# One register load per expert tile, and block 3's attention products traced ahead of block 2's tiles

## The chip, the cores and the metric

The kernel runs on one core of a Trainium2 chip, as one program in one launch. The metric is device time in microseconds (us): the median of repeated executions of the whole program. The kernel before takes 2506.33 us (five runs, 2505.71 to 2507.92).

The core has five engines that run side by side, each with its own instruction queue that is worked off in order: TensorE (PE: matmuls and transposes; its weight loads are listed as PEld), VectorE (DVE), ScalarE (ACT), GpSimd (POOL) and SyncE (SP). SP computes nothing: its queue reads registers and issues DMAs, which 16 DMA engines then carry out. POOL issues the indirect DMAs, those whose row numbers come from a tile.

## The reference

The input is x, 16 sequences of 128 tokens with 256 features. Four blocks follow each other; each adds a cross-attention to a context and then a feed-forward part, both gated by a tanh, both on the layer-normed x:

```
x = x + tanh(g_xattn[l]) * xattn_l(layernorm(x), ctx)
x = x + tanh(g_ffn[l])   * ffn_l(layernorm(x))
```

In blocks 2, 3 and 4 the feed-forward part is a mixture of experts: a router gives every token its K best experts (K = 2 of 8, 4 of 16, 8 of 64), and the token gets the weighted sum of these experts' outputs. One expert of block 2 or 3 is

```
h = silu(x @ Wg) * (x @ Wu)      # 256 -> 176
y = h @ Wd                       # 176 -> 256
```

Block 3's attention has 16 heads of 128 features and normalises queries and keys. Its output is the sum over the heads of attn @ v @ Wo, and since v = ctx @ Wv, the product Wv @ Wo of each head can be formed once from the weights alone. Everything is float32.

## The kernel before, in words

The functions run in the order of the blocks: xattn0, ffn0, xattn1, ffn1, xattn2, ffn2, xattn3, ffn3 (names count from 0; this text counts blocks from 1). The parts that matter are ffn1 (block 2's experts), xattn2 (block 3's attention) and ffn2 (block 3's experts).

**Routing.** While an attention part is running, `Routed.pieces` is worked off beside it, for two sequences at a time: layer norm, transposes (L460, copied by ACT at L468), logits (L158), the best K experts (L171 to L174), places in the experts' lists (L212, L213), target rows (L236), and then K indirect DMAs per sequence from POOL's queue (L240), which send each token's row to its experts' lists in DRAM (`xs_f`). The last pair of sequences is only done after the attention, in `r.finish()`.

**The tile table.** `sparse_experts` (L979 on) counts the tokens of each expert, and computes for each tile of 128 rows its expert and its first row: `tab` has one tile per partition and two columns. It is cast to integers in `tabi` (L1014). The expert number of every tile is also spread over all partitions, by a matmul against the identity (L1019) and a copy (L1021), as `ebc`.

**The tile loop.** There are 39 tiles in ffn1 and 79 in ffn2. Each tile goes through six steps that are staggered over the loop's turns:

- `load` (L1028): SP reads two registers from `tabi`, the expert (L1029) and the row (L1030), each with a check of its bounds; then it issues the load of the expert's up weights `wgu` (L1032, 352 KB, 5 buffers) and of the rows `xe` (L1034, 131 KB in ffn1, 134 KB in ffn2, 4 buffers)
- `load_down`: SP issues the load of the down weights `wdn` (L1040, 176 KB, 5 buffers), one turn later
- `turn`: PE transposes `xe` (L795), DVE copies the result to `xeT` (L1047) and finds the rows to send the results to (L262, L267, L269)
- `up`: matmul (L1054), ACT's silu (L1056), DVE's product (L1058)
- `turn_back`: PE transposes h (L1065), ACT copies it (L1067)
- `down`: matmul (L1074), DVE's weighting (L1076), POOL's indirect DMA of the result rows (L273)

The order of the queues of SP and PE is the written one inside the loop (`manual_schedule`). Everywhere else a planner orders each queue at compile time, by its own estimates and with the order of the program as priority: it may put an instruction far ahead of its place in the program as soon as its inputs and buffers are there. In the attention parts the queues of PE, DVE and ACT are written out by hand and those of SP and POOL are left to the planner.

In ffn2 the loop also carries the shared expert's work: `others` is a list of 40 pieces, the first 12 of which (`ahead`) are traced before the loop and the others spread over its turns. In ffn1 this list is empty.

**Between ffn1 and xattn2.** `xattn2` (L1143) begins with its weights: `wa` (Wq, 2 MB), `wc` (Wk, 1 MB), `wd` (Wv transposed, 1 MB in two halves, L1148), `wb` (Wo, 2 MB), then the 16 products of Wv and Wo in place (`value_products`, matmul at L570, ACT's copy back at L571, two PSUM banks by turns). Then it fetches the experts' results, which the last tiles must have sent (`fetch`, L281), adds them to x (L287), takes the layer norm and begins its own loop with L1163. Block 4 uses the tile `wd` again, for a constant (the load `wd<-in_sums`).

## Time and profile before

| what | value |
|---|---|
| median of five runs | 2506.33 us |
| the profiled execution: its own time | 2522.49 us |
| its span, first to last instruction | 2520.5 us |
| PE busy | 2029.3 us (81%) |
| DVE busy | 1486.2 us (59%) |
| mean granted PE clock | 0.909 of full speed |
| `wgu` loads of the two tile loops | 118 of 352 KB |
| PE busy in ffn1's tiles (811 to 944 us) | 111.72 of 133 us |
| PE busy in ffn2's tiles (1571 to 1831 us) | 244.49 of 260 us |

The page gives, for one profiled execution, the busy time of each engine and the granted PE clock in 40 slices of the span. The trace behind it can be asked for any stretch: which instruction ran when, what an engine's idle time ended with ("waits"), and the busy time of each engine in a list of stretches. Register reads, checks and DMA issues on SP are not counted as busy, but the trace lists each with its start and duration, so SP's queue has to be read from there. In the name of a load, the tile stands left of the arrow and its source right of it. Each float32 matmul of this kernel shows as two MATMUL records.

### The profile page before, as it was taken

The numbers are of one execution on the slowest core, as the hardware profiler recorded it, in microseconds if no ns is written. First come the engines' busy times: TensorE is split into PE (matmuls) and PEld (weight loads), VectorE is DVE, ScalarE is ACT, GpSimd is POOL, SyncE is SP. The second block draws the span as 40 slices with busy tenths as digits, with TensorE's granted clock in tenths as the row PEclk, the third lists the DMA queues.
The fourth block names the chain that finished last, engine by engine and source line by source line (L and its number), as shares of the span: only waits on it lengthen the run. The fifth ranks groups of instructions, "written<-read, shape, count | busy, mean of one in ns | idle before, by whom it ended". The sixth has DMA issues, their size and how long they took to land. (4 is left out here: it accounts for less than half of the span.)

```text
span 2520.5 us, 38199 instructions
## 1 busy us (share of the span) xinstructions
PE 2029.3 (81%) x12988; PEld 1421.4 (56%) x12988; DVE 1486.2 (59%) x4176; ACT 880.3 (35%) x1868; POOL 805.0 (32%) x799
## 2 busy tenths in 40 slices
PE   8999998798886886998999997999946877643760
PEld 5777764366564553665666664666635656533550
DVE  4676764488785444667666664555557745332438
ACT  3433333376562223454444442222223333111320
POOL 1121111243453232334444443223221144444430
PEclk9999999799897998999999998999978888666995
DMA  5169971129002771001000003787722011115768
GB/s 174 67 133 237 271 196 34 51 75 342 14 23 85 241 219 37 17 1 32 16 27 16 16 27 118 228 248 244 237 69 75 1 56 56 65 70 180 248 206 296
DMA packets 198528, 299.32 MB, mean 119 GB/s; under 512 B 21513, under 2 KB 151024, under 8 KB 195904
## 3 DMA queue, kind: packets, MB, share of 16 engines
q1 hardware_dynamic: 175776, 238.90, 33.1%
q0 software_dynamic: 19488, 55.31, 5.9%
q10 hardware_dynamic: 3072, 2.68, 0.3%
q8 instruction: 105, 1.72, 0.3%
q14 instruction: 87, 0.71, 0.1%
HBM read 160.92 MB, written 135.90 MB: 118 GB/s over the span
## 5 line engine op out<-in xcount | busy, mean ns | idle before, releaser
L548 POOL TENSOR_TENSOR e<-e,r 128x512 f32<-128x512 f32 x128 | 133.0, 1039 | 565.8 <-DVE r L547 284.9
L273 POOL DMA_INDIRECT y_f<-ys,drow x182 | 175.0, 961 | 399.2 <-DVE ys L1076 199.1
L240 POOL DMA_INDIRECT xs_f<-hx,hrow x224 | 221.8, 990 | 115.6 <-issue 56.8
L536 ACT ACTIVATE e<-e 128x512 f32<-128x512 f32 x128 | 80.7, 630 | 476.0 <-DVE e L533 476.0
L1054 PE MATMUL mm<-wgu,xeT 128*128 128x352 f32 x472 | 166.6, 476 | 8.7 <-DVE xeT L1047 6.0
L1163 PE MATMUL qk<-wa,xnT 128*128 128x512 f32 x256 | 130.0, 631 | 23.4 <-DVE nq L1177 23.3
L543 DVE TENSOR_REDUCE sm<-e 128x4 f32<-128x512 f32 x128 | 87.8, 686 | 93.2 <-ACT e L536 92.4
L795 PE MATMUL tr<-cst,xe 128*128 128x128 f32 x364 | 72.6, 282 | 79.4 <-DMA wgu<-in_L_gu 46.0
L1074 PE MATMUL o<-wdn,hT 88*128 88x256 f32 x472 | 122.7, 382 | 2.0 <-ACT hT L1067 2.0
L667 PE MATMUL y<-wb,aT 128*128 128x256 f32 x512 | 121.1, 379 | 1.0 <-DVE x_sb L415 1.0
L1216 PE MATMUL y<-wb,aT 128*128 128x256 f32 x512 | 120.9, 379 | 0.0
L667 PEld LDWEIGHTS y<-wb,aT 128*128 128x128 f32 x512 | 97.1, 190 | 41.8 <-issue 18.0
L633 PE MATMUL mm<-xnT,wm 128*128 128x512 f32 x256 | 120.0, 593 | 0.0
L795 PEld LDWEIGHTS tr<-cst,xe 128*128 128x128 f32 x364 | 46.2, 144 | 125.4 <-issue 93.4
L390 POOL TENSOR_TENSOR rr<-ss,nhalf 128x8 f32<-128x8 f32 x64 | 106.0, 1656 | 31.7 <-DVE ss L1171 31.6
L287 DVE TENSOR_TENSOR x_sb<-x_sb,yg 128x256 f32<-128x256 f32 x224 | 93.4, 423 | 32.7 <-DMA yg<-y_f 20.5
L1177 DVE TENSOR_TENSOR nq<-qk,rr 128x512 f32<-128x512 f32 x64 | 44.3, 692 | 113.2 <-POOL rr L390 113.2
L873 DVE TENSOR_REDUCE mx<-sc 128x4 f32<-128x512 f32 x128 | 84.6, 681 | 39.6 <-PE sc L866 39.6
L1067 ACT COPY hT<-tr 88x256 f32<-88x256 f32 x118 | 43.5, 368 | 183.3 <-PE tr L1065 183.1
L1054 PEld LDWEIGHTS mm<-wgu,xeT 128*128 128x128 f32 x472 | 81.8, 193 | 43.1 <-DVE xeT L1047 14.9
L521 PEld LDWEIGHTS tr<-cst,e 128*128 128x128 f32 x512 | 63.4, 141 | 69.9 <-issue 60.8
L1516 PE MATMUL mm<-xeT,wgu 128*96 128x128 f32 x512 | 71.7, 284 | 35.9 <-ACT ys L1530 24.2
(287 smaller groups left out, 4845.4 us busy)
## 6 DMA issues: line engine op xcount, KB each, us to landing
wgu<-in_L_W SPq DMA_DIRECT2D x118, 352.0 KB
xs_f<-zeros SPq DMA_DIRECT2D x32, 1072.0 KB
wdn<-in_L_W SPq DMA_DIRECT2D x118, 176.0 KB
xs_f<-zeros SPq DMA_DIRECT2D x16, 1048.0 KB
y_f<-zeros SPq DMA_DIRECT2D x16, 1024.0 KB
yg<-y_f SPq DMA_DIRECT2D x16, 1024.0 KB
wgu<-in_L_gu SPq DMA_DIRECT2D x64, 192.0 KB
xe<-xs_f SPq DMA_DIRECT2D x79, 134.0 KB
```

The lines of the kernel that those rows point to most:

```text
L240: ins = nc.gpsimd.indirect_dma_start(out=self.rows, out_offset=bass.IndirectOffsetOnAxis(ap=h["row"][:, j, k : k + 1], axis=0), in_=h["x"] ...
L273: self.net.unordered("y_" + self.name, self.net.nc.gpsimd.indirect_dma_start(out=self.y, out_offset=bass.IndirectOffsetOnAxis(ap=row, axis ...
L287: self.net.nc.vector.tensor_tensor(x, x, yg[:, k, :], ALU.add)
L390: return self.nc.gpsimd.tensor_tensor(out, var, self.nhalf[:, :n], ALU.pow)
L548: nc.gpsimd.tensor_tensor(e, e, r.unsqueeze(2).to_broadcast([P, 4, S]), ALU.mult)
L633: nc.tensor.matmul(mm, wm[:, kk, 4 * hq + j, :], self.xnT[:, kk, g * 512 : (g + 1) * 512], start=kk == 0, stop=kk == 1,)
L667: nc.tensor.matmul(y, a[:, j, :], wn[:, 4 * hq + j, :], start=j == 0, stop=j == 3)
L795: self.nc.tensor.transpose(tr[:, kk, :], src[:, kk * P : (kk + 1) * P], self.ident)
L1054: nc.tensor.matmul(gu, xeT[:, kk, :], wgu[:, kk, :], start=kk == 0, stop=kk == 1)
L1074: nc.tensor.matmul(y, hT[:, c, :], wdn[:, c, :], start=c == 0, stop=c == 1)
L1163: nc.tensor.matmul(q, self.xt(kk, b), wq[:, kk, cols], start=kk == 0, stop=kk == 1)
L1216: nc.tensor.matmul(y[b], a[:, j, :], wn[:, h, :], start=h == 0, stop=h == 15)
```

## The change

It has two parts.

**The register load.** The table is turned: `tabi` becomes one row on one partition, with expert and row of each tile side by side. For this a second small matmul against the identity turns the row column (`rp`), and two copies on one partition fill `tabi` from PSUM. In the loop one load instruction reads both registers of a tile, and the checks of their bounds are left out.

**The products.** Block 3's attention weights are loaded in a new function `weights2`, called at the start of `ffn1`, and the 16 products become `others` of ffn1's `sparse_experts` with `ahead` 16: they are traced after the tile table and ahead of the tile loop, with the PSUM banks `sc`, two of them.

```diff
-        tabi = self.sb(pool, "tabi", [P, 2], I32)
-        nc.vector.tensor_copy(tabi, tab)
...
+        rp = self.psum("mm", [1, T])
+        nc.tensor.matmul(rp, tab[:, 1:2], self.ident[:, 0:T], start=True, stop=True)
         ep = self.psum("mm", [P, T])
         nc.tensor.matmul(ep, wide, self.ident[:, 0:T], start=True, stop=True)
+        tabi = self.sb(pool, "tabi", [1, T, 2], I32)
+        nc.vector.tensor_copy(tabi[:, :, 1], rp)
+        nc.vector.tensor_copy(tabi[:, :, 0], ep[0:1, :])
...
         def load(i, _):
-            ev = nc.sync.value_load(tabi[i : i + 1, 0:1], min_val=0, max_val=E - 1)
-            rv = nc.sync.value_load(tabi[i : i + 1, 1:2], min_val=0, max_val=E * NT)
+
+            _, (ev, rv) = nc.values_load_multi_w_load_instructions(
+                tabi[0:1, i, :], engines=(mybir.EngineType.SP,), min_val=0, max_val=E * NT,
+                skip_runtime_bounds_check_because="the table's entries are clamped to the bounds",
+            )
+            ev = nc.s_assert_within(ev, 0, E - 1, skip_runtime_bounds_check_because="clamped to E - 1")
...
     def ffn1(self):
+        self.weights2()
+        products = [partial(self.value_product, "sc", self.w2[2][:, h, :], self.w2[3], h) for h in range(16)]
         with self.tc.tile_pool(name="f1", bufs=1) as one, self.tc.tile_pool(name="f1s", bufs=3) as sp:
-            self.sparse_experts(one, sp, self.t["L1_W1"], self.t["L1_W2"])
-    def xattn2(self):
+            self.sparse_experts(one, sp, self.t["L1_W1"], self.t["L1_W2"], products, 16)
+    def weights2(self):
         nc, t = self.nc, self.t
-        wq = self.weight("wa", t["L2_Wq"].rearrange("(k p) n -> p k n", p=P), [P, 2, 2048])
-        wk = self.weight("wc", t["L2_Wk"], [P, 2048])
         wvT = self.sb(self.wpool, "wd", [P, 16, P])
...
         wo = self.weight("wb", t["L2_Wo"].rearrange("(h p) n -> p h n", p=P), [P, 16, D])
-        wn = self.value_products("qk", wvT, wo, lambda h: h)
+        wq = self.weight("wa", t["L2_Wq"].rearrange("(k p) n -> p k n", p=P), [P, 2, 2048])
+        wk = self.weight("wc", t["L2_Wk"], [P, 2048])
+        self.w2 = wq, wk, wvT, wo
+    def xattn2(self):
+        nc, t = self.nc, self.t
+        wq, wk, _, wn = self.w2
```

## The prediction

> **What bounds the kernel now.** I read the table of stretches first: engine by engine, the busy time in block 2's tiles (between 811 and 944 us) and in block 3's (1571 to 1831 us). Columns: stretch, length, busy PE, PEld, DVE, ACT, POOL, then granted PE clock, DMA share, GB/s.

> ```profile
> 811.00:823.00 12.00, 10.53 (x29) 6.15 (x29) 4.53 (x18) 2.97 (x6) 0.00 (x0) 0.62 0.73 222
> 823.00:923.00 100.00, 83.65 (x373) 55.12 (x371) 48.91 (x186) 21.05 (x62) 29.79 (x31) 1.00 0.81 247
> ...
> 1571.00:1831.00 260.00, 244.49 (x1076) 167.66 (x1074) 137.87 (x484) 58.33 (x165) 74.76 (x78) 1.00 0.77 235
> ```

> No engine is full in block 2's tiles: PE is at 84% at full clock, DMA at 0.81. In block 3's tiles PE is at 94%. The waits say what PE lacks in block 2, between 811 and 932 us; the second line is SP's own, at the head of the loop:

> ```profile
> PE tr L795 <- DMA xe<-xs_f: 15.1, 20, 1.9
> ...
> SPq L1034 <- DMA xs_f<-hx,hrow: 3.5, 1, 3.5
> ```

> PE waits 15.1 us, in 20 tiles, for rows that come late. Late because SP asks late: the timeline of SP's queue shows one tile after the other without a pause for a buffer.

> ```profile
> 869.63 0.35 SPq L1040 DMA_DIRECT2D wdn<-in_L_W  x1
> 871.59 0.34 SPq L1032 DMA_DIRECT2D wgu<-in_L_W  x1
> 872.18 0.33 SPq L1034 DMA_DIRECT2D xe<-xs_f  x1
> 872.75 0.35 SPq L1040 DMA_DIRECT2D wdn<-in_L_W  x1
> 874.70 0.34 SPq L1032 DMA_DIRECT2D wgu<-in_L_W  x1
> ```

> One tile costs SP 874.70 - 871.59 = 3.11 us; with stops for buffers the mean from tile 2's wgu (812.94) to tile 38's (930.44) is 117.5/36 = 3.26. The gaps hold the register loads; the listing by line gives their parts (duration min/median/max in ns, start of first and last) for 869 to 875 us:

> ```profile
> L1029 SPq TENSOR_LOAD <-tabi x2: 492/500/507, 870.0 to 873.1; - x2
> L1029 SPq FUSED_REGOPS  x2: 152/154/155, 870.6 to 873.7; - x2
> ...
> L1030 SPq TENSOR_LOAD <-tabi x2: 274/277/280, 870.8 to 874.0; - x2
> L1030 SPq FUSED_REGOPS  x2: 157/157/157, 871.2 to 874.3; - x2
> ```

> From 870.0 to the next load's registers at 871.4 it is 1.4 us, nearly half of SP's turn. What PE could do without SP is at the loop's end, when every load has been issued:

> ```profile
> 930.17 0.38 PE L795 MATMUL tr<-cst,xe 128*128 128x128 f32 x2
> 930.39 1.03 PE L1074 MATMUL o<-wdn,hT 88*128 88x256 f32 x4
> 931.26 0.38 PE L1065 MATMUL tr<-cst,h 128*88 128x128 f32 x2
> 931.77 1.45 PE L1054 MATMUL mm<-wgu,xeT 128*128 128x352 f32 x4
> 933.06 0.38 PE L795 MATMUL tr<-cst,xe 128*128 128x128 f32 x2
> ```

> A turn is 2.89 us here (933.06 - 930.17), of which 0.39 is PE's weight load waiting for xeT, as the timeline says. So block 2's tiles are **SP-bound at 3.26 against 2.89**, and block 3's, which carry 28 pieces more for PE, are PE-bound with little idle.

> **Part 1, the register load.** *What SP saves.* Gone are one of two loads, both register operations and both assertions. At most it saves all but one load of 0.50: 0.9. At least nothing, if the second register costs its 0.28 again and the register operations stay. I take the nearest row, the first load's 0.50 plus 0.05 of gap, for the load of two, and the checks as gone: 1.4 - 0.55 = 0.85, so SP's turn becomes 3.26 - 0.85 = 2.41, no longer the bound.

> [...] The trace gives 0.50 and 0.28 for two single ones. [...]

> *What is late next.* PE's turn (2.89 as in the tail; 2.50 if DVE does xeT first and the 0.39 goes) or the DMA engines: at a share of 0.81 a tile takes 3.26, so at 1.00 it would take 0.81 x 3.26 = 2.64. I take 2.8, between 2.64 and 2.89.

> *Block 2.* The first transposes of the 39 tiles run from 810.48 to 935.95: 125.47 us, of which the first two turns (3.69 and 3.66) are at the clock of 0.62 and stay. New: 7.35 + 36 x 2.8 = 108.15. **Gain 17.3 us.** With 2.89 it is 14.1, with 2.64 it is 23.1. If only the second load's 0.3 goes, SP's 2.96 sets it: 125.47 - 7.35 - 36 x 2.96 = 11.6.

> *Block 3.* SP leads PE by its buffers here; PE's waits for xe are 7.1 us, 10 times, between 1560 and 1835. Part of that PE gives back to DVE's chain. **Gain 5 us**, ends 0 and 7.1.

> *The table.* Added per loop: a matmul and two copies, less one cast. By L1019 at the low clock (0.65 us) and L1021 (0.20): 0.65 + 2 x 0.20 - 0.17, and the wide copy (0.22) and both hand-overs now lie before SP's first read: some 1.7 us later. In block 2 this is hidden, since SP then stands 3.5 us for the scattered rows; in block 3 because PE works on shared pieces until 1570.8, while the first wgu is issued at 1551.28. **0 us**; without this cover 3.4 for both.

> **Part 2, the products.** *Taken from behind block 2's tiles.*

> ```profile
> 944.17 9.31 PE L570 MATMUL qk<-wb,wd 128*128 128x256 f32 x32 [0.58 <-DVE ys L1076]
> ...
> 947.66 5.06 SPq L281 DMA_DIRECT2D yg<-y_f  x4
> ...
> 960.52 0.72 PEld L460 LDWEIGHTS tr<-cst,xn 128*128 128x128 f32 x4 [7.44 <-DVE xn L447]
> ```

> The 9.31 us look like a stretch on the path, but PE then idles for 7.04 until the layer norm's rows come. Their chain goes past PE: last result rows sent by POOL at 944.39, fetched by SP at 947.66, added by DVE until 956.4, statistics, power on POOL, rows at 960.06. ACT is done with the products at 953.9 and first needed at 961.68. **0 us saved**; no gain, because nothing in that chain waits for them.

> [...]

> *Put ahead of block 2's tiles.* All 32 records need about 9.3 us at full clock. PE is busy 6.65 of 17 us from 786 to 803, and 0.52 of the 8 after it; the work fits, at a clock of 0.60 and 0.50. What it can hit is the routing of the last pair (L460 at 792.01, L158 at 793.85, L212 at 797.80), which ends in the scatter that the first xe waits for. Block 3's head shows the planner putting such pieces between these steps: there the second pair of L460 came 2.28 us after the first. Here a piece is one product, two records of 128x256, 0.96 at half clock (four of L1074's took 1.92 at 926.45), at three stops: +2.9; a PE kept busy does L158 in 0.96 instead of 1.88 and L460 in 0.63 instead of 1.11: -1.4. **+1.5 us**, ends -2 (the first two tiles at 2.8 too) and +15 (all in front, at half clock).

> *The weights.* Written earlier, but the planner has already put them at 400.07 (wb), 454.21 (wa), 457.90 (wd) and 91.0 (wc): 0 us. Behind the products hangs the load of the constant into wd (now 953.51). If it moves ahead of the tiles, SP's queue stands there until the last product is done, covered by the 3.5 us above.

> **Sum.** -17.3 - 5 + 0 + 0 + 1.5 = -20.8. The profiled execution takes 2522.49, its span 2520.5 and 1.99 around it; after: span 2499.7, time 2501.7. The median of the runs without a profile is 2506.33, 16.2 below the profiled time; the difference is carried over: **2485.5**.

> **Rivals.**
> - *DMA is the limit.* For: the share is the same 0.8 in both loops, and an xe takes 4.0 us to land (869.06 to 873.05) where the first took 2.2. Against: SP's queue hardly ever waits, and its instructions follow each other. A turn of 3.1 gives 125.47 - 7.35 - 111.6 = 6.5, block 3 nothing, +1.5: 2501.3.
> - *The load of two saves little.* 11.6 and 2 in block 3, +1.5: 2494.2.
> - *The products stand in front of the routing.* For: PE works in order and the planner fills gaps. Against: their priority is behind the routing's. +9.3 to +15 instead of +1.5: 2493 to 2499.
> - *The load of two is dearer than two loads* (the slower side). L1029's longest load took 0.965; two such are 1.93. It decides from a stretch over 1.4 us. At 0.5 more, SP's turn is 3.76 in block 2 (+18), 3.6 against 3.29 in block 3 (79 x 0.3 = +24), +1.5: 2550. Against: the second load took only 0.28.
> - *The products are not moved by the planner, or SP's loads not fused:* the first leaves 2484, the second 2508.

> **Chances.** Forecast case 0.52 (2476 to 2490), little saved 0.15, products in front 0.10, DMA 0.13, dearer load 0.05, not fused or anything else 0.05. About 0.2% (5 us) can be told from no change: faster 0.83 (the first three and half of DMA's), same 0.11, slower 0.06. The range reaches from 2476 (23.1 + 7.1 gained) to 2500, which leaves out half of DMA's case, the dearer load and the rest.

> **What would show it.** One TENSOR_LOAD per tile on SP of about 0.5 us and no assertions; SP's turn at 2.4, then stopping for buffers; PE's waits for xe under 4 us in block 2 and transposes 2.6 to 2.9 apart; DMA share near 0.9; the gap of 944 to 960 as long as now, without L570; the first xe issued within 2 us of 808.23. I am wrong if xe waits stay with SP ahead (DMA), if SP's turn stays above 2.9, or if the first xe is 5 us late.

## The result, and the profile after

The changed kernel is **slightly slower**: 2514.0 us at the median of 52 executions against 2509.76 of 91 of the kernel before on the same chip, a ratio of 1.0021 (95% interval 1.0013 to 1.0029). Forecast were 2485.5 us (2476 to 2500) with a chance of 0.06 for slower. The profiled execution took 2519.32 us, its span 2517.1.

Read by stages, it is two opposite results. The first transpose of an `xe` (L790 now, L795 before) and the last one bound each tile loop:

| stretch | before | after | difference |
|---|---|---|---|
| up to block 2's first transpose | 810.5 | 801.0 | -9.5 |
| block 2's tiles, first to last transpose | 125.5 | 106.5 | **-19.0** |
| from there to block 3's first transpose | 634.8 | 635.3 | +0.5 |
| block 3's tiles, first to last transpose | 253.1 | 280.2 | **+27.1** |
| the rest | 696.6 | 694.1 | -2.5 |

The first row is not the change's: in the runs below the same stretch took 797 to 805 us, with the products moved and without. It goes with the granted clock, which was 0.945 in it in the profile before and 0.966 in the one after. Of the programs without the products, PE was busy in this stretch for 715.3 us here, at 0.945, and in the runs below for 711.4 at 0.949 and 708 at 0.953 to 0.955. Without that row the profiled pair is near the medians: +6.1 against +4.2.

**Block 2's tiles went as forecast.** The table of stretches (length, busy PE, PEld, DVE, ACT, POOL, granted clock, DMA share, GB/s), two stretches of block 2's tiles and then block 3's, all after the change:

```profile
801.00:813.00 12.00, 10.82 (x28) 6.30 (x28) 3.94 (x18) 2.60 (x5) 0.00 (x0) 0.56 0.88 269
813.00:907.00 94.00, 92.70 (x414) 63.02 (x413) 51.36 (x208) 23.64 (x69) 32.59 (x34) 1.00 0.95 288
1543.00:1830.00 287.00, 253.49 (x1076) 174.85 (x1074) 128.93 (x482) 58.25 (x165) 74.58 (x78) 0.96 0.70 213
```

In block 2 PE rose from 84% to 92.70 of 94 us: it is the bound now, at a turn of 2.70 (median of the transposes' distances), and DMA follows close at 0.95. In block 3 the opposite happened: PE fell from 94% to 88%, and the DMA share from 0.77 to 0.70. SP's register load, from the listing by line for 860 to 872 us, and its queue after it:

```profile
L1028 SPq TENSOR_LOAD <-tabi x5: 697/744/752, 859.5 to 870.6; - x5
```

```profile
866.22 0.34 SPq L1034 DMA_DIRECT2D wgu<-in_L_W  x1
866.82 0.32 SPq L1036 DMA_DIRECT2D xe<-xs_f  x1
867.39 0.35 SPq L1042 DMA_DIRECT2D wdn<-in_L_W  x1
869.07 0.34 SPq L1034 DMA_DIRECT2D wgu<-in_L_W  x1
```

One load of 0.74 us instead of two (0.50 and 0.28), no register operations behind it and no assertions. The turn here is 2.85 us (869.07 - 866.22), but SP now stops for buffers within it, so this is no longer its own speed. That shows at the loops' heads, where SP stops for no buffer: the issues of `wgu` follow each other every 2.31 to 2.33 us there, against 2.98 to 3.01 before.

**The gap behind block 2's tiles is as long as it was**, as forecast: 26.7 us from the last transpose (907.5) to the first L1173 (934.23), against 26.7 before, with the products gone from it. The timeline shows the chain that keeps it:

```profile
915.75 0.96 POOL L273 DMA_INDIRECT y_f<-ys,drow  x1 [0.90 <-DVE ys L1078]
...
919.01 9.33 SPq L281 DMA_DIRECT2D yg<-y_f  x6
...
931.63 0.73 DVE L447 TENSOR_SCALAR xn<-x_sb,mv,rs 128x256 f32<-128x256 f32 x2 [1.30 <-POOL rs L390]
...
932.15 2.29 PE L460 MATMUL tr<-cst,xn 128*128 128x128 f32 x8 [17.20 <-DVE xn L447]
```

PE waits 17.20 us for the rows of the layer norm, where before it waited 7.44 and had done 9.31 us of products.

**Block 3's tiles lost more than block 2's gained.** The page, which counts the whole program, has a new group, the row of the store's destinations (busy, mean ns of one, idle before and its cause), and PE's up matmul shows idle time (before: 8.7):

```profile
L1056 PE MATMUL mm<-wgu,xeT 128*128 128x352 f32 x472 | 174.2, 494 | 33.8 <-DVE xeT L1049 33.2
...
L269 DVE TENSOR_SCALAR drow<-dw,cst 128x1 uint32<-128x1 f32 x182 | 38.8, 213 | 152.0 <-DMA y_f<-ys,drow 142.7
```

VectorE's waits in block 3's tiles (total, times, longest), after:

```profile
DVE drow L269 <- DMA y_f<-ys,drow: 99.6, 60, 3.3
DVE xeT L1049 <- PE tr L790: 33.0, 29, 2.7
```

and before:

```profile
DVE xeT L1047 <- PE tr L795: 17.0, 22, 1.2
...
DVE drow L269 <- DMA y_f<-ys,drow: 9.6, 12, 2.0
```

One such wait in the timeline after:

```profile
1641.01 0.15 DVE L267 TENSOR_REDUCE dw<-eq 128x2 f32<-128x8 f32 x1
...
1641.81 0.38 PE L790 MATMUL tr<-cst,xe 128*128 128x128 f32 x2
...
1643.87 0.21 DVE L269 TENSOR_SCALAR drow<-dw,cst 128x1 uint32<-128x1 f32 x1 [2.71 <-DMA y_f<-ys,drow]
1644.00 0.42 DVE L1049 COPY xeT<-tr 128x256 f32<-128x256 f32 x1
...
1644.47 1.45 PE L1056 MATMUL mm<-wgu,xeT 128*128 128x352 f32 x4 [1.19 <-DVE xeT L1049]
```

The transpose is done at 1642.2, but its copy `xeT` stands behind a `drow` in VectorE's queue, and `drow` waits for a store. PE gets its operand some 1.7 us late.

Why a store? `drow` has six buffers, used in turn. The scattered store of tile i-6 reads its row while it runs, so row i can only be written when that store has landed. In the trace after, the 60 waiting rows of block 3 began 3.4 us (median; 3.1 to 3.9 for the middle 80%) after the end of the issue of store i-6, and that issue takes 0.96: by this a store holds its row for some 4.4 us, an estimate. In the kernel before, the 61 rows that did not wait came 7.2 us (median) after it. What moved is the row's place in VectorE's queue. The order in which the two traces show the instructions, three turns of block 3, numbers relative to tile 31 (eq, drow: destination; h: product; ys: scaling, behind which POOL stores):

```
before: xeT(0) eq(1) ys(-3) drow(1) xeT(1) h(0) ys(-2) eq(2) drow(2) xeT(2) h(1) ys(-1) eq(3) drow(3) h(2)
after:  xeT(0) ys(-3) eq(3) xeT(1) h(0) ys(-2) drow(3) xeT(2) h(1) eq(4) ys(-1) drow(4) h(2) eq(5) drow(5)
```

Before, row 3 comes behind ys(-1), two scalings after ys(-3), whose store must have landed. After, it comes behind ys(-2), one scaling after, and ahead of xeT(2). Not every turn has this order, but the count over the loop says the same. Of the 73 rows from tile 6 on, 57 came behind the scaling of tile i-4 before the change, and none of these waited for a store; the other 16 came behind that of i-5 or i-6, and 12 waited. After, all 73 came behind that of i-5 (60 rows, 48 waited) or i-6 (13 rows, 12 waited). The loop's hand-written order holds SP and PE; VectorE's is the planner's.

### The profile page after: what moved, and what is told of

It is laid out like the page before. It is cut to its first block, busy times and chain, and to the rows that moved or that the text cites. A ratio compares the mean times of both kernels' runs of the same rounds, so it can differ in the third digit from the quotient of the medians.

```text
span 2517.1 us, 37642 instructions
## 1 busy us (share of the span) xinstructions
PE 2024.3 (80%) x12992; PEld 1423.1 (57%) x12992; DVE 1475.3 (59%) x4178; ACT 878.7 (35%) x1868; POOL 803.5 (32%) x799
## 4 chain that ended last, share of the span: by engine, by line
DVE 20%; PE 16%; issue 12%; DMA 9%; POOL 6%; ACT 4%; another core or an unknown queue 2%; SPq 0%; POOLq 0%; DVEq 0%; ACTq 0%
DMA y_f<-ys,drow 5%; POOL rr L390 4%; DVE x_sb L287 3%; DVE ss L1180 2%; POOL y_f L273 2%; DMA yg<-y_f 2%; PE mm L1056 2%; DVE e L533 2%; DVE sm L543 1%; DVE nq L1187 1%; ACT e L536 1%; PE mm L1526 1%; DVE mx L532 1%; PE sc L1374 1%
## 5 line engine op out<-in xcount | busy, mean ns | idle before, releaser
L1056 PE MATMUL mm<-wgu,xeT 128*128 128x352 f32 x472 | 174.2, 494 | 33.8 <-DVE xeT L1049 33.2
L1173 PE MATMUL qk<-wa,xnT 128*128 128x512 f32 x256 | 129.0, 627 | 24.1 <-DVE nq L1187 24.0
L269 DVE TENSOR_SCALAR drow<-dw,cst 128x1 uint32<-128x1 f32 x182 | 38.8, 213 | 152.0 <-DMA y_f<-ys,drow 142.7
L1076 PE MATMUL o<-wdn,hT 88*128 88x256 f32 x472 | 124.9, 388 | 2.0 <-ACT hT L1069 2.0
L790 PE MATMUL tr<-cst,xe 128*128 128x128 f32 x364 | 72.4, 282 | 54.3 <-DMA xe<-xs_f 54.2
L790 PEld LDWEIGHTS tr<-cst,xe 128*128 128x128 f32 x364 | 50.4, 146 | 91.9 <-issue 78.8
```

What stands on the lines that cost most here:

```text
L790: self.nc.tensor.transpose(tr[:, kk, :], src[:, kk * P : (kk + 1) * P], self.ident)
L1056: nc.tensor.matmul(gu, xeT[:, kk, :], wgu[:, kk, :], start=kk == 0, stop=kk == 1)
L1076: nc.tensor.matmul(y, hT[:, c, :], wdn[:, c, :], start=c == 0, stop=c == 1)
L1173: nc.tensor.matmul(q, self.xt(kk, b), wq[:, kk, cols], start=kk == 0, stop=kk == 1)
```

## The experiments

They ran on three other chips than the pair above (1 to 4 on one, 5 to 8 on one, 9 and 10 on one), which were granted a higher clock in the attention behind block 3's tiles (0.78 to 0.80 instead of 0.74); the kernel before takes 2452 to 2455 us on them. Times are therefore compared as ratios to the kernel before on the same chip.

**1. The load alone.** The kernel before with the changed table and load:

```
-            ev = nc.sync.value_load(tabi[i : i + 1, 0:1], min_val=0, max_val=E - 1)
-            rv = nc.sync.value_load(tabi[i : i + 1, 1:2], min_val=0, max_val=E * NT)
+            _, (ev, rv) = nc.values_load_multi_w_load_instructions(tabi[0:1, i, :], ...)
...
```

> The one register load per tile alone (with its new table); weights and products of block 3 stay where the kernel before has them. Theory (VectorE's queue): in block 3's tiles the destination row of tile i is written ahead of the copies of the two tiles before it, so it waits for the scattered store of tile i-6, which still reads the old row; that comes with the register load alone. So block 2's tiles are 19 us shorter, block 3's tiles 27 us longer, as in the changed kernel, and the 9.5 us of block 2's head are not there: about 2523 us, 0.5% above the kernel before, the drow line again with some 100 us of waits in block 3's tiles. Rival (the early weights or products disturb block 3): block 3's tiles stay at 253 us, the time is about 2491.

Measured: 1.0004 (0.9989 to 1.0019). Block 2's tiles 105.4, block 3's 276.5, with 95.7 us of waits of `drow` on stores in them. Both halves of the result come with the load and its table; the theory holds, and the rival (253 and 2491) does not. The expected 0.5% was too much by what the head was thought to be worth. In the trace, VectorE's order in block 3's tiles is the one of the changed kernel; that of experiment 2 is the one of the kernel before.

**2. The products alone.** The changed kernel with the old table and the two loads.

> The weights and products of block 3 moved, two register loads per tile as before. Theory: only the head of block 2's tiles is shorter (9.5 us, the products keep TensorE and its queue busy while the last pair is routed), both tile loops as before (125.5 and 253 us): about 2500 us, 0.4% below. Rival (products cost block 3): block 3's tiles near 280 us and about 2527. If the 9.5 us come from the register load instead: 2509, no change.

Measured: 0.9999 (0.9984 to 1.0014). Block 2's tiles 124.9, block 3's 255.7, first transpose 802.2. Moving the products shows no worth either way, within 0.15% (3.7 us). My 9.5 us for the head were wrong: see experiment 6.

**3. Twelve rows.** In the changed kernel:

```
-        dw = net.sb(self.sp, "dw", [P, 2], bufs=6)
+        dw = net.sb(self.sp, "dw", [P, 2], bufs=12)
-        row = net.sb(self.sp, "drow", [P, 1], U32, bufs=6)
+        row = net.sb(self.sp, "drow", [P, 1], U32, bufs=12)
```

> The changed kernel with 12 instead of 6 buffers of the destination rows and of their sums (dw), nothing else. Theory: a row is then written when the store of tile i-12 is long done, so the waits of drow on the stores (99.6 us in block 3's tiles) go to under 10 us, block 3's tiles take 253 us or less (27 us gained or more) and the kernel about 2485 us, 1% below the kernel before. Rival (transfers: with cheaper loads SP sends earlier, the stores and loads collide, and the waits are only where that shows): the wait moves to another line (eq on xe, or ys on its buffers), block 3's tiles stay near 280 us and the time near 2514.

Measured: **0.9836** (0.9813 to 0.9858). Block 3's tiles 244.2, without a wait of `drow` on a store; the group in that stretch, with its idle time last:

```profile
L269 DVE TENSOR_SCALAR drow<-dw,cst 128x1 uint32<-128x1 f32 x76 | 16.2, 213 | 2.2
```

The rival is out: the transfers could carry more (share 0.81 in this stretch, 0.71 in the changed kernel), and what was late were rows' buffers. More was gained than expected, since block 4's tiles, which call the same function, fell as well, to 132.2, from between 142.4 and 146.0 in runs 1, 2 and 5.

**4. The order held.** The changed kernel with six rows, and one word more:

```
-        with self.tc.manual_schedule(engines={mybir.EngineType.SP, mybir.EngineType.PE}):
+        with self.tc.manual_schedule(engines={mybir.EngineType.SP, mybir.EngineType.PE, mybir.EngineType.DVE}):
```

> The changed kernel with VectorE's order in the tile loops written out as well (each tile's copy, then its destination, in the order of the steps), six row buffers as before. Theory: the row of tile i is written one tile after the place where it stood in the changed kernel, behind the copy of tile i, three tiles' scalings behind; so no waits of drow on stores in block 3, block 3's tiles at 253 us or less and about 2485 us. It can cost a few us where the held order is a worse one for the other work in VectorE's queue: 2480 to 2497. Rival (transfers collide): near 2514 again.

Measured: **0.9831** (0.9803 to 0.9858). Block 3's tiles 238.4, block 4's 145.9 as before. Every row now stands behind its own tile's copy and the scaling of tile i-4. This takes the wait away without a buffer more: six rows are enough where a row stands behind the scaling of tile i-4, and too few where it stands behind that of i-5. PE in block 3's tiles:

```profile
1528.00:1768.00 240.00, 237.42 (x1057) 166.88 (x1056) 133.61 (x486) 56.82 (x161) 71.89 (x75) 1.00 0.84 260
```

It is busy for 237.4 of 240 us at a granted clock of 1.00: what is left of this loop is PE's own work. The held order also shortened the stretch from block 2's last transpose to block 3's first, which took 627 to 628 us in experiments 4, 7 and 10 against 633 to 635 in all other runs; the 7 us are gone between the last L1173 and block 3's first tile, and why was not tried.

**5. The changed kernel once more.**

> The changed kernel itself, for its profile and time on the same chip as the others. Theory: block 2's tiles 20 us shorter and block 3's tiles 24 to 27 us longer than in the kernel before: 0.2% above it; the first transpose of block 2's tiles near 802 us, as in the runs with the load alone and with the products alone. Rival (load and products together gain what neither gains alone): 0.3% below or better.

Measured: 1.0028 (1.0016 to 1.0039). Block 2's tiles 105.0, block 3's 272.2 with 98.9 us of waits of `drow`. The first result stands on a second chip; load and products together make nothing that the load alone does not.

**6. Twelve rows in the kernel before** (the edit of experiment 3).

> The kernel before with 12 buffers of the destination rows and of dw. Theory: in blocks 2 and 3 its rows hardly waited (9.6 us of waits in block 3's tiles, none in block 2's), in block 4 they did (50.8 us): block 2's tiles 125 us as they were, block 3's 247 to 253, block 4's near 133 instead of 146 to 148: 14 to 20 us less, a ratio of 0.992 to 0.994. So about 25 us of the 43 that the changed kernel with 12 rows is faster are the change's own. Rival (more rows do it all, whatever the loads): 0.984 here too. The first transpose of block 2 tells whether its head is 8 us longer without the products (810) or not (802).

Measured: 0.9947 (0.9932 to 0.9963). Block 2's tiles 124.2, block 3's 251.1, block 4's 130.2. So the rows help the kernel before almost only in block 4, where 50.8 us of waits stood already. First transpose at 800.6 without the products: the head does not depend on them.

**7. Both cures.** The changed kernel with the edits of experiments 3 and 4.

> The changed kernel with VectorE's order held in the tile loops of blocks 2 and 3 and with 12 buffers of the rows and of dw. Theory: the two cures meet in block 3 and only the rows act in block 4: block 3's tiles 238 us as with the held order, block 4's 132 as with the rows: 14 us under either alone, a ratio near 0.978. Rival (the transfers or the loads of SP take over): 0.983, with the DMA share at 0.9 and the waits of eq or xeT on xe in place of the others.

Measured: **0.9771** (0.9758 to 0.9785), the fastest run: 2398.47 us against 2453.11. Block 3's tiles 238.4, block 4's 133.0, both as expected.

**8. Eight rows.** The changed kernel with 8 buffers of `drow`, `dw` left at 6.

> The changed kernel with 8 instead of 6 buffers of the destination row alone (dw stays at 6). A store has landed some 3.4 us after its issue; in the changed kernel row i is written 3.4 us after the store of tile i-6 at the median, waiting, and never under 4.7 us after that of tile i-7. Theory: with the store of tile i-8 to wait for nothing waits, block 3's tiles at 244 and block 4's at 132 as with 12, a ratio near 0.984. Rival (the sums dw or a longer reach count too): 0.99 or more.

Measured: 0.9826 (0.9805 to 0.9846). Block 3's tiles 243.7, block 4's 129.8, no row waits for a store. Two buffers more, of one number per partition each, are as good a cure as twelve (0.9836 on its chip), and `dw` has no part in it.

**9. Four rows in the kernel before.**

> The kernel before with 4 instead of 6 buffers of the destination row, nothing else: the same mechanism brought into the kernel that did not have it. Theory: row i waits for the store of tile i-4, which in block 2 was issued after the last scaling before it on VectorE; scaling to landing is about 4.4 us (0.96 of issue and 3.4 after it), the row and the next scaling take some 0.6, so a turn cannot be under 5.0 us: block 2's tiles 38 x 5.0 = 190 instead of 125; in block 3 half of the rows stand behind one scaling more and cost nothing, the other half a turn of 5.0: 290 to 310 instead of 253; block 4 longer by 30 to 90. A ratio of 1.05 to 1.09. Rival (the row's wait covers a limit that is there anyway, such as the transfers): under 1.02.

Measured: 1.0278 (1.0249 to 1.0307). Both expectations missed the ratio. Block 2's tiles went from 125 to 148.9 and block 3's to 287.0, but block 4's stayed at 148.6. The waits of the row in block 2's tiles, where there were none before:

```profile
L269 DVE TENSOR_SCALAR drow<-dw,cst 128x1 uint32<-128x1 f32 x37 | 7.9, 214 | 82.6 <-DMA y_f<-ys,drow 82.5
```

The mechanism is there, and the size was off: in block 2 a waiting row began 2.1 us (median) after the issue of its store, not 3.4, so a turn took 3.8 and not 5.0 us. The landing time was not the same in both loops: in block 3's tiles of this run it was 2.8 us. Block 4 has another order in this trace: 62 of its 64 rows come behind the copy `xeT` of tile i-1, where with six buffers 52 come two copies earlier, behind that of i-3. Its waits for stores stayed at 50.6 us. So the planner gives way to fewer buffers in one loop and not in another (block 2's order is that of the kernel before); that this is why block 4 lost nothing was not tested.

**10. Both cures in the kernel before.**

> The kernel before with VectorE's order held in the tile loops and 12 buffers of the rows and of dw: what the change is worth when the rows hold nobody. Theory: SP's turn with two loads and three issues (3.1 us) is then what binds in both loops: block 2's tiles 125, block 3's 243 to 250, block 4's 131, a ratio of 0.990 to 0.995, so that the change is worth 1.3 to 1.8% beside the changed kernel with the same two cures (0.977). Rival (block 3 gains only from the held order): 238 in block 3 here too, and the change is worth block 2's 20 us alone, 0.8%.

Measured: 0.9921 (0.9897 to 0.9945). Block 2's tiles 124.9, block 3's 252.5, block 4's 131.5. Block 3 stays at 252.5 with the held order, a little over the theory's 243 to 250, and the rival's 238 is out: its 14 us there come from the load. With both cures in both kernels, the change is worth 0.9921 - 0.9771 = 1.5%, of which the spans show 18.2 us in block 2's tiles and 14.1 in block 3's.

## Why the prediction was wrong

- **Block 2: right.** Forecast 17.3 us of gain, measured 19.0 in the first pair and 19.5 between the runs of the load alone and the products alone. SP was the bound; behind it PE came first at 2.70 a turn (forecast 2.8), with DMA at 0.95 just after. The rival that DMA is the limit (6.5 us of gain) fell.
- **The register load: right in effect, mis-sized in its part.** I took 0.50 for the load of two; it takes 0.70 at the median over all 118. The two singles were 0.78 together, so the load itself saves under 0.1, and the rest of what SP saves is the checks and their gaps. By these medians the load of two takes 0.20 more than the first of the singles did. At the loops' heads the whole saving was some 0.7 a tile and not 0.85 (2.31 to 2.33 against 2.98 to 3.01). That cost nothing here, since PE's 2.70 was reached all the same.
- **Block 3: this step failed.** "Block 3. Gain 5 us, ends 0 and 7.1" became a loss of 27.1. The prediction read PE's waits for `xe` and counted what could go of them. It did not ask what holds VectorE's queue in this loop, although SP's and PE's orders alone are fixed there. With the new load the planner put the rows one scaling and one to two copies earlier, and six buffers no longer reached. Experiments 3, 4 and 8 take that away, each by another edit or another size, and then block 3's tiles take 244, 238 and 244. Beside the kernel before with the same edits (251 with twelve rows, 252.5 with both) that is a gain of 7 and 14 us, at my far end of 7.1 and beyond it. So the forecast's own quantity was there, and was turned into a new wait.
- **How the 27 us come about.** PE's idle time in block 3's tiles went from 253 - 238.5 = 14.5 to 280 - 247.5 = 32.5 us, 18 more; and its busy time grew by 9 at a granted clock of 0.96 instead of 1.00.
- **The gap behind block 2's tiles: right**, 0 saved (26.7 and 26.7).
- **The products ahead: +1.5 forecast, nothing that can be told from noise measured** (0.9999, within 0.0015 or 3.7 us, which leaves room for 1.5 and none for the far end of 15). They went into PE's idle time: ahead of block 2's first transpose PE is idle for 91 to 95 us in the five traces without them and for 84 to 88 in the seven with them. The load of the constant into `wd` did move ahead and SP stood 12.1 us behind the products, as the working feared; SP still waited 3.5 us for the scattered rows after that, so it was covered.
- **The table: 0 forecast**; the load alone with its table shows no cost at block 2's head (802.7 against 802.2 with the old table), though the spread of that stretch, 797 to 805 us, would hide the 1.7.
- **The rivals.** The slower side was given to one mechanism, a dear register load. The case that came was not among them: a buffer that is read by a transfer long after the engine that filled it has gone on (a store held its row for some 4.4 us, by the estimate above). It could have been seen. The trace of before has `drow` waiting for `y_f` in block 3's tiles, 9.6 us, and in block 4's, 50.8. A wait that small in a loop that one is about to make faster shows how near the limit is.

What stays open: why the planner moves the rows. That it does so with the load and its table, and not with the products, is in the orders that the traces show (experiments 1 and 2); whether the shorter load, the missing checks or the new table moves it was not tried.

## What to carry to other kernels

When a change makes one queue of a loop faster, look at every queue whose order is not written out: the planner may reorder it, and the new order has to be checked against the number of buffers of each small tile that a transfer reads. In these traces a waiting row was written once the store that read its buffer had landed, 3.4 us (median) after the end of its issue in block 3's tiles (after), so add two counts: by how many tiles the row runs ahead of the last scaling, and how many turns of the faster loop a store takes to land. An estimate from the numbers above: rows that stand behind the scaling of tile i-5 or i-6, and stores that take 4.4 us, or 1.6 turns of 2.7, need 6.6 or 7.6 buffers. Six were too few and eight were enough; seven was not run. Rows behind that of i-4, at 1.5 turns of 2.88, need 5.5, and six did. Here eight rows instead of six turned +0.3% into -1.7%. And before a stretch of a profiled pair is credited to an edit, find its spread: the 9.5 us of the head were not the edit's.

## What the runs showed of the hardware

PE's granted clock fell five times inside block 3's tiles of the kernel after, and PE was at work in the 3.4 us before each fall, for 1.0 to 1.6 us. Three neighbouring stretches:

```profile
1654.70:1658.10 3.40, 1.02 (x6) 0.61 (x4) 0.07 (x2) 0.71 (x2) 0.00 (x0) 1.00 0.70 225
1658.10:1661.50 3.40, 2.84 (x6) 1.74 (x7) 1.03 (x4) 0.09 (x1) 0.96 (x1) 0.50 0.49 173
1661.50:1664.90 3.40, 3.40 (x18) 2.58 (x17) 2.01 (x8) 0.92 (x3) 0.96 (x1) 1.00 0.14 53
```

The time for which a scattered store holds the tile with its row numbers was not constant either: its issue takes 0.96 us on POOL in both loops, but a row that waited for it began 3.4 us (median) after that in block 3's tiles (after), and in experiment 9 2.8 us after it in block 3's and 2.1 in block 2's.
